# Attention and routed experts on one core: the last batch's attention interleaved with the first sort, and the order of writes and fillers changed

## The chip, the cores and the metric

One NeuronCore of a Trainium2 chip runs the whole kernel. The metric is the device time of one execution in microseconds; lower is better. The engines are TensorE (PE), VectorE (DVE), ScalarE (ACT), GpSimd (POOL) and SyncE (SP). DMA transfers are issued from the queues of SP, ACT and POOL, and each engine carries out its own instructions strictly in the order in which the program lists them.

## What is computed

The input is x (4 batches of 256 rows, 256 columns, float32), a context of 4 x 256 x 128 and two gates. Two residual steps follow each other:

```python
query = ctx @ Wq.T + bq;  key = ctx @ Wk.T + bk
attention = softmax(query @ key.T)
x = x + tanh(g_xattn) * (layernorm(x) @ attention.T)      # per batch

z = layernorm(x)
probs = softmax(gelu(z @ rw1) @ rw2)                      # 8 experts
wgt, idx = top_k(probs, 2)
for e in range(8):
    Ye = gelu(z @ w1[e] + b1[e]) @ w2[e] + b2[e]          # 256 -> 1024 -> 256
    Ce = gelu(b1[e]) @ w2[e] + b2[e]
    for k in range(2):
        mask = idx[..., k] == e
        out += any(mask) * wgt[..., k] * where(mask, Ye, Ce)
x = x + tanh(g_ffn) * out
```

Since a row that did not choose an expert still gets Ce, the kernel adds the same constant to every row (the sum of active * Ce, weighted by the row's two weights) and lets the experts' rows contribute Ye - Ce. The difference is made in the hidden layer: gelu(b1) is subtracted from gelu(z w1 + b1) before the second product.

## The kernel before

**First stage** (the text `order`, L433). Batches 0, 1 and 2 (1024 rows in all are 8 tiles of 128; these are tiles 0 to 5) go through attention, layer norm and router. Each word of `order` is a step from the table `steps` (L428), such as `qk:1` (the projections of batch 1) or `xf:2a` (normalize tile 4). The schedule is manual: the order of the words is the order on every engine. The steps that the change touches: `st` (L303, bn_stats for the first layer norm, VectorE), `pw`/`pf` (L306, L351, its power -0.5 on POOL), `xn` (L309, normalize), `tra`/`xnT` (transposes on TensorE, copy on ScalarE), `en`, `nmax`, `exp`, `norm`, `pt`, `attT` (energy, row maximum, exponential, division by the sum, transposes and their copy), `po` (product of attention and normalized rows), `add` (L342, residual, and the write of the rows to the output), `sf`/`xf` (second layer norm; `xf`, L354, also writes the normalized rows to the scratch `rows` in DRAM), `trf`, `xT`, `r`, `gel`, `lg` (router), `chosen` (which two experts a row takes). `w2:n` puts the next n loads of w2 (1 MB each) on SP's queue. Tanh, Exp and Gelu need different activation tables on ScalarE, and a table is loaded when a function needs it that the present one lacks.

**First sort.** The 1536 (row, expert) pairs of tiles 0 to 5 are sorted by expert into slots of 128 pairs of one expert each. NA = 5 full slots can be filled before batch 3 is known. `cnt`, `pc`, `scan`, `over`, `runs`, `lead`, `rank`, `pos`, `split`, `put` count and place the pairs with small VectorE instructions and TensorE products; `hqs_inv` (12 one-hot compares on VectorE, 24 small products on TensorE) turns the positions into the slots' lists; `lists` makes row numbers of them, `past` and `who` the expert of each slot, `sel` and `bias_` the slots' biases. `soft`, `wgt` and `piece` make the softmax weights. Batch 3's attention steps are placed between these (L910 to L920).

**Slots.** For each slot, POOL gathers 128 normalized rows from `rows` (L745), TensorE transposes them (`turn`, L753; the copy xs is on ScalarE for slots 0 to 4, on VectorE after), `first_layer` (L768, here F0, F1 ...; F1.3 is its fourth chunk of eight) multiplies by w1 of the slot's expert, which SP has loaded (`fill`, 1 MB, six buffers), ScalarE applies Gelu and VectorE subtracts gelu(b1). `second_layer` (L790, here S0, S1 ...) multiplies by w2, VectorE scales the result (ys) and POOL adds it to the output rows by an indirect DMA (L801). TensorE runs F0, turn 1, turn 2, F1, S0, turn 3, F2, S1, and so on. Tiles 6 and 7 are sorted with what the first sort left over (second sort, slots 5 on); this data uses 19 slots, of which 16 are in the fixed part and the rest under branches.

**Fillers.** After every chunk of F or S the function `between` (L957) is called with 0.45 of credit (less after the chunks that carry VectorE work). It takes the next items of two lists and puts their instructions at that place in every queue: `main` (L932: batch 3's router, second sort, biases, then the bias path: for each expert e a row b2 is loaded into one of two buffers by `b2_`, L811, and eight `bias_path` and two `both_` instructions on VectorE add up the constants; `sums1_`, L854, sums them over partitions with one TensorE product called cst; then `constant_row` for each tile and `add_constants`) and `second` (L954: the weights of the first sort's slots). A number in a list is a break of so many calls. Items with a cost wait until the credit is not negative.

A few lines carry the rest of the working:

```python
    def hidden(name, shape=(P, IC, P), dtype=F32):                                   # L461
        return slotp.tile(list(shape), dtype, tag="hT", bufs=6, name=name)
        go.hqs = hidden(f"hqs{i}", (P, go.ng, P), BF16)                              # L627
        if e < 2:                                                                    # L813
            nc.gpsimd.memset(b2_row[e], 0.0)
        nc.sync.dma_start(out=b2_row[e % 2][0:1, :], in_=b2[e : e + 1, :])
            if s > NA:                                                               # L978
                gather_to(s + AHEAD)
            if 0 < s < NA - 2:
                fill_to(s + 2)
```

`slotp` is opened after the pools of the first stage have been closed and lies in their memory.

Of the kernel before, what the change touches and what calls it, by code (L numbers as in the profile page):

```python
# [19 lines left out]
def gated_xattn_moe_kernel(  # L20
# [25 lines left out]
    P = 128  # L46
# [105 lines left out]
    nc.gpsimd.dma_start(out=g_sb, in_=gates[0].partition_broadcast(P))  # L152
# [105 lines left out]

    def norm(b):
        att, den = live["att", b], live["den", b]  # L260
        rden = small.tile([P, NN], F32, tag="rden", name=f"rden_{b}")
        nc.vector.reciprocal(rden, den)
        for m in range(NN):
            nc.vector.tensor_scalar(  # L264
                att[:, m, :], att[:, m, :], rden[:, m : m + 1], tg[:, 0:1], ALU.mult, ALU.mult
            )
# [26 lines left out]
    def normal(kind, key, tiles, dst):  # L293
        mv, rstd = live["ln", kind + key]
        for i, t in enumerate(tiles):
            nc.vector.tensor_scalar(
                dst[:, i, :], acc[:, t, :], mv[:, i, 0:1], rstd[:, i : i + 1], ALU.subtract, ALU.mult
            )
# [10 lines left out]
    def xn(b):  # L309
        normal("a", b, rows_of(b), made("xn", b, [P, LT, D]))  # L310
# [31 lines left out]
    def add(g):  # L342
# [3 lines left out]
        nc.sync.dma_start(out=in_rows(total, g), in_=xb)  # L346
# [61 lines left out]
    def tbl(_):  # L408

        nc.scalar.activation(warm, ones[:, 0:1], AF.Tanh)  # L410

# [12 lines left out]

    def w2_(n):
# [5 lines left out]
        chosen=chosen, tbl=tbl, ident=ident_, masks=masks, w2=w2_,  # L431
    )
    order = """  # L433
        w2:5 tbl ident qk:0 st:0 qk:1 tg q:0 k:0 pw:0 st:1 qk:2 k:1 q:1 xn:0 pw:1 st:2 en:0 k:2 q:2 tra:0 nmax:0 pw:2
        en:2 xnT:0 xn:1 exp:0 en:1 nmax:2 tra:1 xn:2 exp:2 norm:0 tra:2 xnT:1 norm:2 pt:0 xnT:2 masks nmax:1 pt:2
        attT:0 exp:1 po:0 attT:2 norm:1 po:2a add:0 pt:1 sf:0 po:2b attT:1 add:2a po:1 pf:0 add:2b sf:2a xf:0 w2:1
        pf:2a add:1 trf:0 sf:2b xT:0 sf:1 pf:2b r:0 gel:0 xf:2b w2:1 pf:1 xf:2a w2:1 trf:2b lg:0 xT:2b trf:2a xf:1
        r:2b xT:2a chosen:0 trf:1 gel:2b r:2a xT:1 lg:2b gel:2a chosen:2b r:1 lg:2a gel:1 chosen:2a lg:1 chosen:1
# [22 lines left out]
    def hidden(name, shape=(P, IC, P), dtype=F32):  # L461
        return slotp.tile(list(shape), dtype, tag="hT", bufs=6, name=name)
# [50 lines left out]
    nc.gpsimd.memset(runs2[:, 0:1], 0.0)  # L513

# [106 lines left out]
    def put_(i):  # L621
# [5 lines left out]
        go.hqs = hidden(f"hqs{i}", (P, go.ng, P), BF16)  # L627
# [43 lines left out]
    def soft_(i):  # L671
# [5 lines left out]
        nc.gpsimd.tensor_tensor(flat, euler.to_broadcast([P, n * E]), flat, ALU.pow)  # L677
# [90 lines left out]
    def first_layer(s, hT, between=nothing):  # L768
# [5 lines left out]
        for ch in range(IC):  # L774
# [13 lines left out]
            between(0.45 - (0.69 if ch % 4 == 3 else 0.0))  # L788

    def second_layer(s, hT, between=nothing):  # L790
# [4 lines left out]
        for i in range(IC):  # L795
            nc.tensor.matmul(ps[:, 0:D], lhsT=hT[:, i, :], rhs=w2_sb[:, i, :], start=(i == 0), stop=(i == IC - 1))  # L796
            between(0.45 - (0.9 if i == IC - 1 else 0.0))
# [111 lines left out]
    with tc.manual_schedule(engines=MANUAL):  # L909
        do("cnt:0 pc:0 scan qk:3 soft:0 over:0 runs:0 lead:0 q:3 k:3 rank:0 pos:0 split:0 en:3 put:0")  # L910
        hqs_inv(0)
        do("past:0 who:0 fill:0 lists:0 gather:0 nmax:3 exp:3 st:3 gather:1 pw:3 gb1 fill:1 sel:0")
        bias_(0, 0, 0, NA)
        do("norm:3 pt:3 xn:3 attT:3 tra:3 xnT:3 gather:2")
        bias_(0, 1, 0, NA)
        do("po:3 wgt:0 add:3")
        for v in range(3):
            piece_(0, v)
        turn(0, transposed_rows(0))
        do("sf:3 pf:3 gather:4 fill:2")  # L920
# [8 lines left out]
        def f(cost, fn, *a):  # L929
# [3 lines left out]
            w(.65, "xf:3"), 2, w(0, "trf:3"), w(0, "xT:3"), 2, w(0, "r:3"), w(0, "gel:3"), 2, w(0, "lg:3"), 1,  # L933
            w(1.6, "chosen:3"), w(.25, "cnt:1"), 2, w(0, "pc:1"), w(.42, "scan"), w(.5, "soft:1"), w(.9, "over:1"),
            w(.35, "runs:1"), w(.8, "lead:1"), w(.5, "rank:1"), w(1.25, "pos:1"), w(.9, "split:1"), w(.6, "put:1"),
        ]
        for g in range(0, G, 4):
# [4 lines left out]
            1, w(.6, "lists:1"), w(.45, "past:1"), w(.6, "who:1"), w(0, "gather:8 fill:7"), w(.25, "sel:1"),  # L942
        ]
        third = XS // 3
        main += [f(1.1, bias_, 1, i, 0, third) for i in range(2)] + [w(1.0, "wgt:1")]
# [121 lines left out]
```

## Time and profile before

| | |
|---|---|
| runs | 216.37, 215.63, 216.63, 213.5 us; median 216.0 |
| profiled execution | 214.05 us, of which the span is 212.3 |
| TensorE busy | 181.7 us (86%), mean granted clock 0.939 |
| VectorE busy | 143.1 us (67%) |
| ScalarE busy | 78.9 us (37%) |
| GpSimd busy | 80.3 us (38%) |
| first h of slot 0 | 53.82 us |
| last ys ends | 204.28 us |

The page divides the span into 40 slices of 5.3 us; a digit is the busy share of a slice in tenths, and the line PEclk is the clock granted to TensorE, 9 being full speed and 5 half. The chain that ended last gives start, length and the work or the wait in order of time. The timeline gives start, length, engine, line, operation and, in brackets, how long the engine had been idle before it and what ended that. SPq, ACTq and POOLq are DMA issues.

### The profile page before, as it was taken

How to read it: one execution, taken by the hardware profiler on the slowest of the kernel's cores; microseconds unless marked ns; L12 is line 12 of the kernel's file. 1: busy time of each engine (PE TensorE's matmuls, PEld its weight loads, DVE VectorE, ACT ScalarE, POOL GpSimd, SP SyncE). 2: the span in 40 equal slices, each digit the busy share in tenths (PEclk: the TensorE clock that was granted, in tenths of full speed). 3: DMA queues.
4: the chain of work that ended last, by engine and by line, in shares of the span. 5: the costliest groups of instructions: out<-in, count | busy, mean ns of one | idle time of the engine just before them, and what ended most of it. 6: DMA issues, size and time to landing. Idle time of an engine off the chain costs nothing.

```text
span 212.3 us, 3829 instructions
## 1 busy us (share of the span) xinstructions
PE 181.7 (86%) x1198; PEld 160.0 (75%) x1198; DVE 143.1 (67%) x419; ACT 78.9 (37%) x205; POOL 80.3 (38%) x89
## 2 busy tenths in 40 slices
PE   3699784728499999699999999999999999999930
PEld 2577472416389989589899999999989989999820
DVE  2777989593637778879858999999988742243200
ACT  2275441071265516135135324532532452354100
POOL 7210314971313507704061246423440430566230
PEclk9999995555999999999999999999999999999995
DMA  5999999157596014990647979759662249332221
GB/s 158 259 321 352 356 373 367 49 170 300 189 304 254 6 23 82 369 277 18 194 104 256 330 260 247 240 183 350 180 206 44 47 48 152 49 55 35 50 29 20
DMA packets 23576, 38.76 MB, mean 183 GB/s; under 512 B 2328, under 2 KB 17696, under 8 KB 23552
## 3 DMA queue, kind: packets, MB, share of 16 engines
q1 hardware_dynamic: 18208, 32.16, 43.8%
q0 software_dynamic: 4912, 6.17, 17.2%
q8 instruction: 13, 0.21, 0.4%
q10 hardware_dynamic: 432, 0.13, 0.3%
q14 instruction: 11, 0.09, 0.1%
HBM read 33.21 MB, written 5.64 MB: 183 GB/s over the span
## 4 chain that ended last, share of the span: by engine, by line
PE 59%; DMA 17%; DVE 11%; issue 6%; POOL 2%; ACT 1%; SPq 0%; POOLq 0%; DVEq 0%; ACTq 0%
PE h L777 25%; PE y L796 23%; DMA out<-ys,give 8%; DMA rows<-xf 4%; DMA xg<-rows,take 3%; DMA ctx_sb<-in_ctxT 3%; PE po L331 2%; PE qk L224 2%; PE xt L760 2%; POOL out L801 1%; DVE att L264 1%; DVE acc L345 1%; DVE nmax L247 1%; DVE st_f L284 1%; DVE hqs L632 1%
## 5 line engine op out<-in xcount | busy, mean ns | idle before, releaser
L781 ACT ACTIVATE hT<-h,bsel 128x128 f32<-128x128 f32 x152 | 55.9, 368 | 74.1 <-PE h L777 56.6
L777 PE MATMUL h<-xs,w 128*128 128x128 f32 x608 | 72.2, 276 | 0.5 <-ACT xs L762 0.5
L777 PEld LDWEIGHTS h<-xs,w 128*128 128x128 f32 x608 | 69.9, 192 | 1.3 <-ACT xs L762 0.7
L796 PE MATMUL y<-w_all,hT 128*128 x304 | 70.1, 381 | 0.6 <-issue 0.6
L796 PEld LDWEIGHTS y<-w_all,hT 128*128 128x128 f32 x304 | 56.0, 190 | 7.7 <-issue 0.9
L801 POOL DMA_INDIRECT out<-ys,give x14 | 22.8, 1630 | 52.5 <-DVE ys L799 29.9
L784 DVE TENSOR_TENSOR hT<-hT,gbsel 128x512 f32<-128x512 f32 x38 | 26.2, 689 | 20.7 <-ACT hT L781 18.8
L823 DVE SCALAR_TENSOR_TENSOR gsum<-w_all,gb,gsum 128x256 f32<-128x256 f32 x56 | 27.1, 484 | 1.6
L745 POOL DMA_INDIRECT xg<-rows,take x23 | 25.3, 1102 | 7.5 <-issue 3.4
L799 DVE TENSOR_SCALAR ys<-y,share 128x256 f32<-128x256 f32 x19 | 9.1, 481 | 14.7 <-PE y L796 11.6
L801 POOL DMA_INDIRECT out<-ys,take x5 | 8.8, 1753 | 22.5 <-DVE ys L799 14.3
L677 POOL TENSOR_TENSOR prob<-euler,prob 128x48 f32<-128x48 f32 (+1 forms) x2 | 10.9, 5468 | 14.6 <-DVE capped L569 7.4
L760 PE MATMUL xt<-ident,xg 128*128 128x128 f32 x40 | 7.8, 278 | 2.3 <-DMA xg<-rows,take 1.8
L291 POOL TENSOR_TENSOR rstd_f<-rstd_f,halves 128x2 f32<-128x2 f32 x3 | 2.1, 712 | 18.7 <-DVE rstd_f L286 18.7
L760 PEld LDWEIGHTS xt<-ident,xg 128*128 128x128 f32 x40 | 5.6, 145 | 4.8 <-issue 2.3
L331 PE MATMUL po<-attT,xnT 128*128 128x256 f32 x24 | 7.8, 478 | 0.7 <-ACT xnT L324 0.7
L224 PE MATMUL qk<-ctx_sb,wq_sb 128*128 128x256 f32 x6 | 3.5, 682 | 5.2 <-DMA ctx_sb<-in_ctxT 5.2
L762 DVE COPY xs<-xt 128x256 f32<-128x256 f32 x15 | 6.3, 418 | 1.6 <-PE xt L760 0.6
L331 PEld LDWEIGHTS po<-attT,xnT 128*128 128x128 f32 x24 | 5.4, 236 | 2.3 <-ACT xnT L324 1.1
L272 PE MATMUL pt<-ident,att 128*128 128x128 f32 x16 | 3.2, 327 | 4.3 <-DVE att L264 4.2
L762 ACT COPY xs<-xt 128x256 f32<-128x256 f32 x5 | 1.9, 371 | 12.5 <-PE xt L760 12.5
L632 DVE TENSOR_SCALAR hqs<-rowb,qf 128x128 bf16<-128x128 bf16 x28 | 4.8, 249 | 2.5 <-DMA rows<-xf 2.5
(200 smaller groups left out, 179.2 us busy)
## 6 DMA issues: line engine op xcount, KB each, us to landing
w<-in_w SPq DMA_DIRECT2D x18, 1024.0 KB, 7.7
w_all<-in_w SPq DMA_DIRECT2D x8, 1024.0 KB, 11.8
acc<-in_x SPq DMA_DIRECT2D x4, 256.0 KB, 5.7
w<-in_w SPq DMA_DIRECT2D x2, 512.0 KB
out<-acc POOLq DMA_DIRECT2D x1, 1024.0 KB
out<-acc SPq DMA_DIRECT2D x3, 256.0 KB, 7.3
rows<-xf SPq DMA_DIRECT2D x3, 256.0 KB
ctx_sb<-in_ctxT SPq DMA_DIRECT2D x3, 128.0 KB
```

The source lines that it names most:

```text
L331: nc.tensor.matmul(ps[:, ts(i, N)], lhsT=live["xnT", b][:, n, ts(t % LT, P)], rhs=live["attT", b][:, n, :], start=(n == 0), stop=(n == NN ...
L677: nc.gpsimd.tensor_tensor(flat, euler.to_broadcast([P, n * E]), flat, ALU.pow)
L745: nc.gpsimd.indirect_dma_start(out=xg, out_offset=None, in_=rows[0 : EARLY * P if s < NA else T, :], in_offset=bass.IndirectOffsetOnAxis(a ...
L760: nc.tensor.transpose(ps[:, ts(c, P)], xg[:, ts(c, P)], ident)
L762: copy(xs, ps[:, 0:D].rearrange("p (c l) -> p c l", c=DC))
L777: nc.tensor.matmul(ps[:, 0:P], lhsT=w1_sb[:, c, ts(ch, P)], rhs=xs[:, c, :], start=(c == 0), stop=(c == DC - 1),)
L781: nc.scalar.activation(hT[:, ch, :], ps[:, 0:P], AF.Gelu, bias=bias[:, ch : ch + 1])
L784: nc.vector.tensor_tensor(hT[:, part, :], hT[:, part, :], gbias[:, part].rearrange("p (i o) -> p i o", o=1).to_broadcast([P, 4, P]), ALU.s ...
L796: nc.tensor.matmul(ps[:, 0:D], lhsT=hT[:, i, :], rhs=w2_sb[:, i, :], start=(i == 0), stop=(i == IC - 1))
L799: nc.vector.tensor_scalar(ys, ps[:, 0:D], go.share[:, j : j + 1], None, ALU.mult)
L801: nc.gpsimd.indirect_dma_start(out=total[0:last_row, :], out_offset=bass.IndirectOffsetOnAxis(ap=go.give[:, j : j + 1], axis=0), in_=ys, i ...
L823: nc.vector.scalar_tensor_tensor(gsums[e], w2_all[:, e, c, :], gb1[:, e, c : c + 1], b2_row[e % 2] if c == 0 else gsums[e], ALU.mult, ALU.add)
```

## The change

1. The gates' load leaves POOL's queue for ScalarE's; the tanh of the gates (`tg`) moves from ahead of `q:0` to behind `q:2`. `tbl` becomes `table:NAME`, which can load any table: Tanh at the start, Exp at the end of the first stage, Gelu ahead of the slots.
2. `add` no longer writes the output rows. A new step `ow` does, and stands at the end of the first stage (for batch 3: behind `add:3`). The last three w2 loads move behind `xf:1`'s write of the normalized rows.
3. Batch 3: `st:3 pw:3 xn:3` move into the first stage (with `xn:3` on POOL), `qk:3`, `q:3`, `k:3` and gelu(b1) to its end, and transposes, energy, maximum, exponential, division and the transposes of the attention between the first sort's steps. Its division is made on ScalarE, by reciprocals that VectorE has multiplied by the gate (`rden`).
4. hqs0 gets memory of its own (`hqs1` in pool `last`); hT has five buffers instead of six.
5. The first sort's exponential is on ScalarE; `soft:0` moves behind the lists.
6. Ahead of slot 0 only slot 0's biases are made; those of slots 1 to 4 go into `second`. `fill:2` is no longer issued ahead of slot 0, and gathers 2 to 4 stand behind `pf:3`.
7. Fillers: other costs, longer breaks in batch 3's router, `past:1 who:1` ahead of the second sort's places, smaller deductions of credit, items of `main` released down to a credit of -1, and marks by which an item must have been put in place.

The diff, cut to its core:

```diff
-    nc.gpsimd.dma_start(out=g_sb, in_=gates[0].partition_broadcast(P))
...
+    def rden(b):
+        live["rden", b] = rden_ = small.tile([P, NN], F32, tag="rden", name=f"rden_{b}")
+        nc.vector.reciprocal(rden_, live["den", b])
+        if b == "3":
+            nc.vector.tensor_scalar(rden_, rden_, tg[:, 0:1], None, ALU.mult)
+
     def norm(b):
+        att = live["att", b]
+        if b == "3":
+            for m in range(NN):
+                nc.scalar.activation(att[:, m, :], att[:, m, :], AF.Copy, scale=live["rden", b][:, m : m + 1])
+            return
+        rden(b)
...
     def xn(b):
-        normal("a", b, rows_of(b), made("xn", b, [P, LT, D]))
+        normal("a", b, rows_of(b), made("xn", b, [P, LT, D]), nc.gpsimd if b == "3" else nc.vector)
...
-        nc.sync.dma_start(out=in_rows(total, g), in_=xb)
+
+    def ow(g):
+        nc.sync.dma_start(out=in_rows(total, g), in_=acc[:, spread(g), :])
...
     order = """
-        w2:5 tbl ident qk:0 st:0 qk:1 tg q:0 k:0 pw:0 st:1 qk:2 k:1 q:1 xn:0 pw:1 st:2 en:0 k:2 q:2 tra:0 nmax:0 pw:2
+        w2:5 table:Tanh g ident qk:0 st:0 qk:1 q:0 k:0 pw:0 st:1 qk:2 k:1 q:1 xn:0 pw:1 st:2 en:0 k:2 q:2 tg tra:0 nmax:0 pw:2
         en:2 xnT:0 xn:1 exp:0 en:1 nmax:2 tra:1 xn:2 exp:2 norm:0 tra:2 xnT:1 norm:2 pt:0 xnT:2 masks nmax:1 pt:2
-        attT:0 exp:1 po:0 attT:2 norm:1 po:2a add:0 pt:1 sf:0 po:2b attT:1 add:2a po:1 pf:0 add:2b sf:2a xf:0 w2:1
-        pf:2a add:1 trf:0 sf:2b xT:0 sf:1 pf:2b r:0 gel:0 xf:2b w2:1 pf:1 xf:2a w2:1 trf:2b lg:0 xT:2b trf:2a xf:1
-        r:2b xT:2a chosen:0 trf:1 gel:2b r:2a xT:1 lg:2b gel:2a chosen:2b r:1 lg:2a gel:1 chosen:2a lg:1 chosen:1
+        attT:0 st:3 pw:3 xn:3 exp:1 po:0 attT:2 norm:1 po:2a add:0 pt:1 sf:0 po:2b attT:1 add:2a po:1 pf:0 add:2b sf:2a xf:0
+        pf:2a add:1 trf:0 sf:2b xT:0 sf:1 pf:2b r:0 gel:0 xf:2b pf:1 xf:2a trf:2b lg:0 xT:2b trf:2a xf:1 w2:3
+        r:2b xT:2a chosen:0 trf:1 gel:2b r:2a xT:1 lg:2b gel:2a chosen:2b r:1 lg:2a qk:3 gel:1 gb1 table:Exp q:3 k:3
+        chosen:2a lg:1 chosen:1 ow:0 ow:2a ow:2b ow:1
     """
...
-        return slotp.tile(list(shape), dtype, tag="hT", bufs=6, name=name)
+        return slotp.tile(list(shape), dtype, tag="hT", bufs=5, name=name)
...
+    hqs1 = last.tile([P, GA, P], BF16, name="hqs1")
...
-        go.hqs = hidden(f"hqs{i}", (P, go.ng, P), BF16)
+        go.hqs = hqs1 if i == 0 else hidden(f"hqs{i}", (P, go.ng, P), BF16)
...
-        nc.gpsimd.tensor_tensor(flat, euler.to_broadcast([P, n * E]), flat, ALU.pow)
+        if i == 0:
+            nc.scalar.activation(flat, flat, AF.Exp)
+        else:
+            nc.gpsimd.tensor_tensor(flat, euler.to_broadcast([P, n * E]), flat, ALU.pow)
...
-            between(0.45 - (0.69 if ch % 4 == 3 else 0.0))
+            between(0.45 - (0.6 if ch % 4 == 3 else 0.0))
...
-            between(0.45 - (0.9 if i == IC - 1 else 0.0))
+            between(0.45 - ((0.4 if s < NA else 0.8) if i == IC - 1 else 0.0))
...
-        do("cnt:0 pc:0 scan qk:3 soft:0 over:0 runs:0 lead:0 q:3 k:3 rank:0 pos:0 split:0 en:3 put:0")
+        do("cnt:0 tra:3 pc:0 scan en:3 xnT:3 over:0 runs:0 nmax:3 lead:0 exp:3 rank:0 pos:0 split:0 rden:3 put:0 norm:3 pt:3 attT:3")
         hqs_inv(0)
-        do("past:0 who:0 fill:0 lists:0 gather:0 nmax:3 exp:3 st:3 gather:1 pw:3 gb1 fill:1 sel:0")
-        bias_(0, 0, 0, NA)
-        do("norm:3 pt:3 xn:3 attT:3 tra:3 xnT:3 gather:2")
-        bias_(0, 1, 0, NA)
-        do("po:3 wgt:0 add:3")
+        do("past:0 who:0 fill:0 lists:0 gather:0 sel:0 soft:0 po:3 gather:1 fill:1")
+        for i in range(2):
+            bias_(0, i, 0, 1)
+        do("wgt:0 add:3 table:Gelu ow:3")
+        turn(0, transposed_rows(0))
+        do("sf:3 pf:3 gather:4")
         for v in range(3):
             piece_(0, v)
-        turn(0, transposed_rows(0))
-        do("sf:3 pf:3 gather:4 fill:2")
...
-            w(.65, "xf:3"), 2, w(0, "trf:3"), w(0, "xT:3"), 2, w(0, "r:3"), w(0, "gel:3"), 2, w(0, "lg:3"), 1,
-            w(1.6, "chosen:3"), w(.25, "cnt:1"), 2, w(0, "pc:1"), w(.42, "scan"), w(.5, "soft:1"), w(.9, "over:1"),
-            w(.35, "runs:1"), w(.8, "lead:1"), w(.5, "rank:1"), w(1.25, "pos:1"), w(.9, "split:1"), w(.6, "put:1"),
+            3, w(.65, "xf:3"), 3, w(0, "trf:3"), 1, w(0, "xT:3"), 3, w(0, "r:3"), w(0, "gel:3"), 3, w(0, "lg:3"), 1,
+            w(1.4, "chosen:3"), w(.2, "cnt:1"), 4, w(0, "pc:1"), w(.35, "scan"), w(.3, "soft:1"), w(.7, "over:1"),
+            w(.3, "runs:1"), w(.5, "past:1"), w(.5, "who:1"), w(.45, "lead:1"), w(.4, "rank:1"), w(1.3, "pos:1"),
+            w(.75, "split:1"), w(.6, "put:1"),
...
-        second = [2] + [f(0, inw_, 0, g) for g in range(GA)] + [1, w(.25, "share:0")]
+        second = [f(.6, bias_, 0, i, 1, 2) for i in range(2)] + ["biases 1"]
+        second += [f(1.2, bias_, 0, i, 2, NA) for i in range(2)] + ["biases 2"]
+        second = [5] + [f(0, inw_, 0, g) for g in range(GA)] + [2, w(.25, "share:0"), "shares 0"] + second
...
+                    if isinstance(queue[0], tuple) and queue[0][0] > 0 and credit < (-1.0 if name == "main" else 0.0):
                         break
```

## The prediction

> **What bounds the kernel now.** I read the page, then the chain that ended last, then the timeline of 20–110 us and of the stretch where the constants are summed, then busy time by windows of 1 us.
>
> From the page:
> ```profile
> span 212.3 us, 3829 instructions
> PE   3699784728499999699999999999999999999930
> PEclk9999995555999999999999999999999999999995
> ```
> From 53 us on TensorE is full but for one notch; before that it has a hole (slices 6 to 11) in which its clock is half. By the windows the clock falls at 32.6 us and is back at 53.1. The chain in order of time shows what fills the hole:
> ```profile
> 30.48 9.21 DMA rows<-xf
> ...
> 39.98 2.04 DVE hqs L632 x12
> ...
> 49.30 3.79 PE po L331 x8
> ...
> 81.91 6.17 DMA xg<-rows,take
> ```
> The first is a false dependency: hqs0 is carved from memory that xf held, so VectorE waits until the last rows have been written (2.51 us idle before 39.98), behind 8 MB of w2 and the output rows on SP's queue. Then batch 3's attention runs alone until slot 0 starts at 53.82. The fourth line is the notch: TensorE waits 1.76 us for the gather of slot 5. From slot 4 on every slot takes 7.25 us of TensorE (118.69, 125.94, 133.18 in the timeline).
>
> A third place matters, the bias path's constants, in the timeline:
> ```profile
> 105.14 0.48 DVE L799 TENSOR_SCALAR ys<-y,share 128x256 f32<-128x256 f32 x1
> 105.90 1.56 POOL L801 DMA_INDIRECT out<-ys,take  x1 [4.96 <-DVE ys L799]
> 107.77 1.01 POOL L745 DMA_INDIRECT xg<-rows,take  x1 [0.30 <-PE h L777]
> 109.08 1.05 POOL L745 DMA_INDIRECT xg<-rows,take  x1 [0.30 <-issue]
> 110.14 0.33 POOL L814 MEMSET b_row<- 128x256 f32 x1
> 110.49 0.29 SPq L815 DMA_DIRECT2D b_row<-in_b  x1
> 111.97 0.49 DVE L823 SCALAR_TENSOR_TENSOR gsum<-w_all,gb,b_row 128x256 f32<-128x256 f32 x1 [2.43 <-issue]
> ...
> 157.51 1.10 PE L856 MATMUL cst<-both,ones 128*128 128x512 f32 x2
> ```
> The second b2 row is cleared on POOL behind a scatter and two gathers, so VectorE stands for 2.43 us. Afterwards it runs late: ys at 121.63 belongs to a product that ended at 118.85 (2.8 us late), ys at 155.76 to one that ended at 155.09 (0.7 late). It has just caught up when cst needs it. No slack is left there.
>
> **Part by part: up to slot 0.** All times are estimates, worked out from rows of before.
>
> st:3 enters VectorE's first stage: 1.33 us (43.24 to 44.57) into a wait of 1.09 (17.72 to 18.80), so +0.25. pw:3 (0.72) and xn:3 go to POOL ahead of pf:0, which starts at 21.83: POOL is free from about 20.0, and pf:0 may start at 22.7 before xf:0 is late, so xn:3 has 2.7 us. POOL runs no such operation before. Bounds: two clears of 128x256 at 0.33 give 0.7 us; two at the rate of the power in L677 (8.01 us for 48 columns) give 85. I take 1.5, nearer the clear, since subtract and multiply are no power; hidden. GPSIMD Engine Reference, section Engine selection, calls POOL the wrong engine here, about twice VectorE's time; twice the 0.41 of a VectorE row would be 1.6 for both, an estimate that fits the hole too.
>
> The gates' load leaves POOL's queue (0.77) for ACT's (0.45), and tg moves from 6.81 to after q:2; ACT idles there and norm:0 needs tg only at 15.26: nothing.
>
> qk:3 goes in front of lg:1 on TensorE. lg:2a ends at 31.1, qk:3 takes 1.8 (9.07 to 10.78), lg:1 0.5: chosen:1 starts at 33.5 instead of 32.04. With the 0.25, +1.45: cnt:0 at 35.0 instead of 33.50. gb1, the Exp table (1.28 + 0.2), q:3 and k:3 on ACT end at 34.0, before en:3.
>
> Then VectorE: scan, over, runs to 36.1 (0.36 less, soft:0 is gone from here); en:3 on TensorE 35.45 to 37.2 (1.70 at full clock, 2.07 at half); nmax to 37.9; lead to split 2.19; rden 0.35; put 0.37: 40.8. The wait for the rows is gone, hqs starts at once: 42.8; past and who: 43.4 (now 42.57). So the sorting does not get shorter: what the wait gave up, qk:3, en:3 and nmax take. norm:3 on ACT and pt:3 end at 42.0, the 24 inv at most 0.085 each later: the list stands at 43.5 to 44.1 (now 42.6). soft:0's power (8.01 on POOL) becomes an ACT exp under 0.5; POOL was idle anyway: nothing.
>
> What follows is shorter. Rows go ahead of w2:3 and the outputs, whose 4.2 MB from 28.3 on at 0.365 MB/us end near 40, before the gather; the four ow issues (0.4 each on SP) end by 33, before fill:0. Gather 0 starts 0.9 after the list (as now, 43.50): 44.6. Now its bytes pass between 47 and 48, 4.7 us after the start, beside the fills: 49.3. Turn and copy 0.95 (52.87 to 53.82): **slot 0 at 50.2, 3.6 earlier.** po:3 (44.0 to 47.8 at half clock), add:3 (0.69), sf:3 (1.27), pf:3 (0.97) lie beside that and end at 50.8; gather 2, now behind pf:3 on POOL (51.0, landing by 54.2), is just in time for turn 2 at 55. ow:3 and the later fill 2 are hidden: fill 2 is due at slot 2.
>
> Clock: now it rises at 53.1, after 3.8 us of po:3. If po:3 does not lift it, F0 runs at half speed for up to 3 us, +1.5 (nothing if it does). I take nothing and keep 1.5 for the range. TensorE: Matmul & The Clock Gate, Part 1, gives a free-running window of 3.4 us, so its phase may differ by run; by that rule about half the runs would pay.
>
> **Slots 0 to 5.** Now slot 1 starts at 63.49 and slot 2 at 71.0, because xf:3 waits for pf:3 (56.42) and PE stops for trf, r, lg in turn. With pf:3 done early and pauses of 3, F0 costs 3.57 + 0.7 (trf, inw); then turn 1, turn 2, and 1.1 for ACT's xT:3 and xs copies: F1 at 56.35. F1 with r and lg 4.85, S0 with pc 3.55, turn 0.2: slot 2 at 65.0 (6.0 earlier). VectorE gets the bias of slots 1 to 4 (2.55 us) here. Its list from add:3 to lists:1 sums to 20.1 us in some 23 of TensorE, so it is nearly the bound: 0.85 is lost before the first inv. Slot 3 at 73.3, the list at 77.0. Gather 5 starts at 77.3; who:1 now stands before the sort's end, so SP issues fills 5 to 7 near 66 and their 3 MB are through by 76 (1 MB in 2.9 us at 0.36 MB/us, the rate of 20 to 30 us); it lands at 80, before turn 5 at 81.0: **the notch of 1.76 is gone**, slot 4 at 81.25 (now 88.62). But piece 2 ends at 85.0 and inw comes at F4.4 (83.5): 1.45 back, what is late next. Slot 5 at 90.6 (96.98), slot 6's turn at 98.0, ys of slot 4 ends at 99.2 (105.62): **6.4 gained there.** One buffer less in hT costs nothing: hqs0 no longer takes one and hT_s is reused five allocations later, when slot s is long over.
>
> **What is given back.** The row's chain after that ys is unchanged: 0.28 + 1.56 + 0.30 + 1.01 + 0.30 + 1.05 + 0.04 + 0.33 + 1.5 = 6.4: b2's row lands at 105.55. From there 70 items at 0.467 (10 more slots' items: a slot of 6.63 has 10, one of 7.03 has 11) and 12.2 of ys, xs and hT: 45 to 45.4 (now 111.97 to 157.36). both is ready at 150.9, 6.4 earlier. But the filler now releases faster: credit per slot is 7.2 - 1.2 - 0.8 = 5.2 instead of 7.2 - 1.38 - 0.9 = 4.92, and main may go to -1, so cst is queued on TensorE after product S11.3 instead of F13.4. TensorE is there at 147.0 (slot 6 at 98.0 + 6 x 7.25, + 5.5) and waits 3.9 us. Behind cst it has 4.2 us more work than now (S11.4 to 7, a turn, F13.0 to 4). Net 6.4 - 4.1 = 2.3 to 2.4. The constant rows and their write then come earlier, and the last scatter's chain (205.14 to 205.88) is the same.
>
> Sum: span 212.3 - 2.4 = 209.9. The profiled execution took 214.05, 1.95 less than the median of the runs, 216.0; the middle of these five executions is 215.6. I set the sum against that: 215.6 - 2.4 = **213.2 us**.
>
> **Rivals.**
> - The early start stays whole: VectorE is not late at cst, since the b2 row lands sooner or the items run faster. For: from 120 to 140 us VectorE is busy 19.36 of 20 us and holds nobody up; against: the row's chain above. 215.6 - 6.4 = 209.2.
> - Nothing to measure: half clock in F0 (1.5) and a gather that lands a microsecond later leave 4 at slot 6, all given back at cst: 215.6. For: from 46 to 50 us TensorE was busy 2.85 of 4 us and the clock stayed at half; against: po:3 follows inv without a gap.
> - Slower: xn:3 on POOL holds up pf:0. It decides from 2.7 us for the pair; each microsecond beyond goes into the VectorE chain, and from 5.1 on the 2.4 are gone. At 4 us each: 8 - 2.7 = 5.3 against 2.4, so 215.6 + 2.9 = 218.5. For: POOL's arithmetic rows are slow (0.72 us for two columns); against: the clears.
>
> **How the numbers follow.** Chances: forecast 0.47, whole gain 0.25, nothing 0.18, slower 0.10. The forecast's own range is 211.5 to 215 (1.5 for the clock, 1.5 to 2 for the waits estimated in slots 1 to 4). For eight in ten I go from 208.3 (the whole gain and 0.9) to 217.5, leaving out the worse half of the slow case and the very best. About 1% (2.2 us) is what a measurement here can tell from no change. Faster by more needs under 213.8: some 0.6 of the forecast's 0.47 (0.28), nearly all of the second (0.24), a little of the third (0.05): 0.57. Slower by more, over 218.2: most of the last and a trace of the third: 0.11. The same: 0.32.
>
> **What would show it.** Right: no wait before hqs; cnt:0 near 35, slot 0's first h near 50, slot 2 near 65; no wait of xt for slot 5; VectorE idle some 4 us before the second b2 row, and TensorE standing 3 to 4 us before cst. Wrong: cst without a wait (then near 209), a first h after 52, or xn:3 beyond 1.3 us each with pf:0 late behind it.

## The result, and the profile after

| | before | after |
|---|---|---|
| median of the runs | 214.17 us (212.5 to 217.57, 70 runs) | 213.53 us (212.05 to 214.34, 44 runs) |
| profiled execution | 214.05 us, span 212.3 | 214.36 us, span 212.5 |
| TensorE busy, mean clock | 181.7 us, 0.939 | 182.1 us, 0.941 |
| GpSimd busy | 80.3 us | 72.6 us |
| first h of slot 0 | 53.82 us | 47.46 us |
| constants' product (cst) | 157.51 us, no wait | 150.71 us, after a wait of 4.66 |

The ratio of the runs is 0.9981, 95% interval 0.9966 to 0.9995: some 0.4 us less, within the 1% that the prediction counts as no change. 213.2 us was predicted; that is near 213.53, but only because the sum was set against 215.6 and the runs of before have their middle at 214.17. The predicted difference, -2.4 us, was several times the measured one, and the predicted span, 209.9, was 2.6 us too short. Some executions of any of these kernels are longer by some per cent; the ratios leave out those more than 1.5% above the fastest of their kernel, the medians do not. The profiled execution of after, 214.36 us, is longer than any of its 44 runs, so the spans and waits read below are those of a long one.

The page of the kernel after, the lines that answer to those shown of before:

```profile
span 212.5 us, 3835 instructions
PE   3999763929899997999999999994699999999940
PEclk9999999557999999999999999999679999999995
```

Counted from 1, the early hole is shorter (slices 6 to 9), the notch of slice 17 is gone, and slices 28 and 29 have a new hole, with a new loss of clock in 29 and 30. That hole holds most of the answer. The timeline of after (start, length, engine, line, operation; in brackets the idle time before it and what ended it), the early stage and the place of the hole:

```profile
18.06 2.45 POOL L304 TENSOR_SCALAR xn<-acc,mv_a,rstd_a 128x256 f32<-128x256 f32 x2
28.90 0.68 PE L223 MATMUL qk<-ctx,wq_sb 128*128 128x256 f32 x2
36.86 2.04 DVE L648 TENSOR_SCALAR hqs<-rowb,qf 128x128 bf16<-128x128 bf16 x12
39.12 3.78 PE L339 MATMUL po<-attT,xnT 128*128 128x256 f32 x8
40.42 1.22 POOL L764 DMA_INDIRECT xg<-rows,take  x1 [14.96 <-DMA out<-acc]
46.34 0.66 PE L779 MATMUL xt<-ident,xg 128*128 128x128 f32 x2 [3.43 <-issue]
47.46 4.59 PE L796 MATMUL h<-xs,w 128*128 128x128 f32 x24 [0.46 <-ACT xs L781]
...
80.30 0.38 PE L779 MATMUL xt<-ident,xg 128*128 128x128 f32 x2
84.08 0.59 PE L727 MATMUL inw<-putw,hqs 128*128 128x54 bf16 x16 [1.17 <-DVE putw L719]
...
105.58 0.48 DVE L842 SCALAR_TENSOR_TENSOR gsum<-w_all,gb,b_row 128x256 f32<-128x256 f32 x1 [4.07 <-DMA b_row<-in_b]
...
144.16 1.89 PE L815 MATMUL y<-w_all,hT 128*128 x8
150.71 2.05 PE L875 MATMUL cst<-both,ones 128*128 128x512 f32 x2 [4.66 <-DVE both L851]
152.55 3.62 PE L815 MATMUL y<-w_all,hT 128*128 x8
```

Read the last three rows first. TensorE stands 4.66 us for VectorE's constants, and then the same eight records of y that took 1.89 us before the wait take 3.62 behind it; cst takes 2.05 (1.10 in the kernel before). The windows of one microsecond say why (the figure before the last two is the granted clock):

```profile
149.00:150.00 1.00, 0.00 (x0) 0.00 (x0) 0.96 (x3) 0.00 (x0) 0.69 (x2) 0.96 0.80 328
150.00:151.00 1.00, 0.29 (x1) 0.32 (x2) 0.56 (x2) 0.00 (x0) 1.00 (x1) 0.50 0.78 136
156.00:157.00 1.00, 1.00 (x7) 1.00 (x6) 0.79 (x3) 0.00 (x0) 0.03 (x1) 0.62 0.00 0
```

The clock falls to half at 149.9, 3.9 us after TensorE's last work, and is back at 156.8. So in these two rows behind the wait 0.95 + 1.73 = 2.7 us are lost to half clock, and in the turn and the first products behind them, up to 156.8, another 0.3: from cst to the start of the next second layer it takes 9.43 us here (150.71 to 160.14), and 6.48 at full clock in experiment 3 (151.09 to 157.57).

**Where the time went, by the starts of the slots' turns on TensorE.** Slot 2 is 6.2 us earlier than before (64.42 against 70.61), slot 5 is 7.9 (80.30 against 88.21), slot 7 is 7.4 (96.78 against 104.19). At cst 4.66 go to the wait and 2.95 to the half clock, and at 175.49 the y waits 0.69 where it waited 0.35: 7.41 - 4.66 - 2.95 - 0.34 = -0.54. The last scatter starts 0.44 later than before (206.32 against 205.88). Of the 7.4 some 1.2 is no work of the change: the second projection started at 7.21 in the profiled execution of before and at 5.67 in that of after, and in a profiled execution of nearly the kernel before (with one clear moved, below) it started at 5.95 and slot 7 at 102.95. Against that one the lead is 6.2. Counted from the second projection, the profiled execution of after is even the longer one by 1.7 us (212.5 - 5.67 against 212.3 - 7.21), while the runs differ by 0.4 the other way: single executions do not settle the last microsecond or two.

### The profile page after: what moved, and what is told of

Its sections match the earlier page's. It is cut to its first block, busy times and chain, and to the rows that moved or that the text cites. A ratio compares the mean times of both kernels' runs of the same rounds, so it can differ in the third digit from the quotient of the medians.

```text
span 212.5 us, 3835 instructions
## 1 busy us (share of the span) xinstructions
PE 182.1 (86%) x1198; PEld 161.5 (76%) x1198; DVE 142.6 (67%) x424; ACT 80.0 (38%) x210; POOL 72.6 (34%) x89
## 4 chain that ended last, share of the span: by engine, by line
DVE 20%; PE 18%; issue 13%; DMA 5%; POOL 2%; SPq 1%; POOLq 0%; DVEq 0%
DVE gsum L842 11%; PE h L796 8%; PE y L815 8%; DVE hT L803 4%; DMA out<-ys,give 4%; DVE both L851 2%; POOL out L820 2%; DVE ys L818 1%; PE cst L875 1%; DVE xs L781 1%; DMA out<-ys,take 1%; DMA b_row<-in_b 1%; PE xt L779 1%; POOL xg L764 0%; SPq L893 0%
## 5 line engine op out<-in xcount | busy, mean ns | idle before, releaser
L796 PE MATMUL h<-xs,w 128*128 128x128 f32 x608 | 74.9, 280 | 0.6 <-ACT xs L781 0.5
L796 PEld LDWEIGHTS h<-xs,w 128*128 128x128 f32 x608 | 72.0, 196 | 1.4 <-ACT xs L781 1.2
L815 PE MATMUL y<-w_all,hT 128*128 x304 | 71.2, 387 | 0.7 <-issue 0.7
L815 PEld LDWEIGHTS y<-w_all,hT 128*128 128x128 f32 x304 | 57.3, 194 | 9.0 <-issue 1.9
L764 POOL DMA_INDIRECT xg<-rows,take x23 | 24.1, 1048 | 22.8 <-DMA out<-acc 15.0
L696 POOL TENSOR_TENSOR prob<-euler,prob 128x16 f32<-128x16 f32 x1 | 2.9, 2934 | 13.6 <-DVE capped L585 13.6
L842 DVE SCALAR_TENSOR_TENSOR gsum<-w_all,gb,b_row 128x256 f32<-128x256 f32 x8 | 3.9, 481 | 4.7 <-DMA b_row<-in_b 4.7
L299 POOL TENSOR_TENSOR rstd_a<-rstd_a,halves 128x2 f32<-128x2 f32 x4 | 3.0, 752 | 11.3 <-DVE rden L260 6.6
L781 ACT COPY xs<-xt 128x256 f32<-128x256 f32 x5 | 1.8, 372 | 13.2 <-PE xt L779 13.2
L851 DVE SCALAR_TENSOR_TENSOR both<-gsum,act,both 128x256 f32<-128x256 f32 x14 | 6.3, 482 | 0.2
```

Of the source, the lines that this page charges most:

```text
L764: nc.gpsimd.indirect_dma_start(out=xg, out_offset=None, in_=rows[0 : EARLY * P if s < NA else T, :], in_offset=bass.IndirectOffsetOnAxis(a ...
L781: copy(xs, ps[:, 0:D].rearrange("p (c l) -> p c l", c=DC))
L796: nc.tensor.matmul(ps[:, 0:P], lhsT=w1_sb[:, c, ts(ch, P)], rhs=xs[:, c, :], start=(c == 0), stop=(c == DC - 1),)
L842: nc.vector.scalar_tensor_tensor(gsums[e], w2_all[:, e, c, :], gb1[:, e, c : c + 1], b2_row[e % 2] if c == 0 else gsums[e], ALU.mult, ALU.add)
L851: nc.vector.scalar_tensor_tensor(both[:, k, :], gsums[e], a, both[:, k, :], ALU.mult, ALU.add)
```

## The experiments

Times are medians of the runs; "ratio" is to the kernel before, run beside it on the same chip (before: 215.04, 214.48 and 214.75 us on three chips). One execution of 374.9 us of the first kernel of the table and one of 471.05 us of the kernel before are left out of these medians. Spans are those of the one profiled execution of each kernel.

| kernel | time | ratio, 95% interval | span |
|---|---|---|---|
| after, both b2 rows cleared early | 206.98 | 0.9597 (0.9483 to 0.9712) | 206.0 |
| after, longer break ahead of cst | 206.56 | 0.9586 (0.9474 to 0.9698) | 205.5 |
| after, TensorE kept busy through the wait | 211.49 | 0.9825 (0.9732 to 0.9918) | 209.8 |
| after, TensorE kept busy ahead of slot 0 | 211.89 | 0.9857 (0.9798 to 0.9916) | 210.8 |
| after, early clear and busy ahead of slot 0 | 204.96 | 0.9548 (0.9506 to 0.9590) | 203.2 |
| the last, and a break of 6 ahead of cst | 205.22 | 0.9578 (0.9530 to 0.9627) | 203.2 |
| after, xn:3 on VectorE | 214.65 | 1.0006 (0.9964 to 1.0048) | 213.1 |
| after, old allowances of the fillers | 218.66 | none (215.06 to 219.67) | 217.8 |
| before, both b2 rows cleared early | 214.38 | 0.9996 (0.9955 to 1.0038) | 211.0 |
| before, gates' load on ScalarE's queue | 214.53 | 1.0015 (0.9967 to 1.0064) | 211.8 |
| before, early rows and own hqs0 | 213.05 | 0.9938 (0.9901 to 0.9974) | 211.8 |
| the last, and soft:0 on ScalarE | 212.12 | 0.9897 (0.9834 to 0.9961) | 210.6 |

**1. The second b2 row.** The theory was that its late load makes the wait at cst.

```diff
-        if e < 2:
-            nc.gpsimd.memset(b2_row[e], 0.0)
+        if e == 0:
+            nc.gpsimd.memset(b2_row[0], 0.0)
+            nc.gpsimd.memset(b2_row[1], 0.0)
```

> The changed kernel, with both b2 buffers cleared on POOL at the first expert, so that the second row's load no longer stands behind a scatter and two gathers. Theory 1 (the start's gain is given back at cst, because VectorE stood 4.07 us for that row): VectorE goes on at 101.4 instead of 105.6, both is ready near 146.4, TensorE waits under 0.7 us ahead of cst, its clock stays up, and the wait of 4.66 and the 2.7 us at half clock behind it are gone: 7 us less than the changed kernel, about 206.5. Rival (VectorE is the bound through the whole bias path, the row's wait only shows it): cst still waits 3 us or more and the time falls by under 2 us.

The timeline of that kernel:

```profile
102.41 0.47 DVE L843 SCALAR_TENSOR_TENSOR gsum<-w_all,gb,b_row 128x256 f32<-128x256 f32 x1
147.55 1.10 PE L876 MATMUL cst<-both,ones 128*128 128x512 f32 x2 [0.53 <-DVE both L852]
```

The row is there without a wait, cst waits 0.53 us and runs at full clock. The span, 206.0, is what the prediction's first rival gives (212.3 - 6.4 = 205.9): with this wait away the early gain stays whole. The rival, VectorE as the bound through the whole bias path, falls.

**2. The place of cst.** The row stays late; TensorE is given other work in front of cst.

```diff
-        main += [2, f(0, sums1_, 0), 2, f(.8, sums2_, 0)]
+        main += [14, f(0, sums1_, 0), 2, f(.8, sums2_, 0)]
```

> The changed kernel with a break of 14 instead of 2 calls ahead of cst, nothing else: the row's wait on VectorE stays, but cst is queued on TensorE some 5.4 us of work later. Theory 1: TensorE does its products meanwhile and does not wait; 7 us less than the changed kernel, about 206.5, the same as with the early clear. Rival (VectorE's backlog is what ends last, wherever cst stands): no change beyond 1 us, since the constant rows come later by as much.

VectorE still stands 4.08 us for the second row, at 105.12, but the timeline has no wait at cst:

```profile
150.96 1.02 PE L875 MATMUL cst<-both,ones 128*128 128x512 f32 x2
```

The clock is 1.00 through the place. So the late row costs nothing by itself; it costs where a product that needs its sum stands too early in TensorE's order.

**3. The wait without the half clock.** Twenty 128x128 products that nothing uses stand on TensorE ahead of cst (here, and where such products come again below, they are work that the reference does not have).

```diff
+        for _ in range(20):
+            nc.tensor.matmul(live["cst", 0][:, 0:P], lhsT=ident, rhs=ones, start=True, stop=True)
```

> The changed kernel with 20 products of 128x128 float32 (some 4.4 us at full clock, their results overwritten) put on TensorE directly ahead of cst. They add work and compute nothing. Theory 1a (the half clock after the wait is caused by the wait, and costs 2.7 us): cst and the four products behind it run at full clock, the time falls by 2 to 3 us, to about 211. Rival 1b (the clock falls for another reason, or its cost is hidden): no gain, or a loss of up to 1 us.

The timeline:

```profile
146.37 4.63 PE L876 MATMUL cst<-ones,ident 128*128 128x128 f32 x40
151.09 1.12 PE L877 MATMUL cst<-both,ones 128*128 128x512 f32 x2
152.05 1.89 PE L815 MATMUL y<-w_all,hT 128*128 x8
```

cst starts no earlier than in the kernel after, but it takes 1.12 us and the eight y take 1.89, at a clock of 1.00. The span is 209.8, 2.7 less. The forecast span was 209.9: this is the kernel that the prediction's sum described, the wait without its aftermath.

**4. Is the row worth anything in the kernel before?** The diff of 1, made to the kernel before.

> The kernel before with both b2 rows cleared at the start of the bias path, so that VectorE no longer stands 2.43 us for the second one. Theory (before, the constants' product stands on TensorE where VectorE has just been in time; the b2 row alone is worth nothing there): 0 to 0.5 us less than before, ratio 0.997 to 1.001, the wait at the second b2 row gone, the constants' product still near 157. Rival (the b2 row's chain is on the path of the kernel before too, so that clearing it early is a gain of its own): 2 to 2.4 us less, ratio 0.989.

Ratio 0.9996. There cst stands behind F13.4 and comes at 156.2 with no wait, so clearing early gains nothing:

```profile
156.19 1.10 PE L857 MATMUL cst<-both,ones 128*128 128x512 f32 x2
```

The span, 1.3 us shorter than that of the kernel before, is the earlier start of this execution (second projection at 5.95 against 7.21). The wait at cst is the change's own.

**5. The old allowances of the fillers,** the prediction's reason for cst having moved forward.

```diff
-            between(0.45 - (0.6 if ch % 4 == 3 else 0.0))
+            between(0.45 - (0.69 if ch % 4 == 3 else 0.0))
-            between(0.45 - ((0.4 if s < NA else 0.8) if i == IC - 1 else 0.0))
+            between(0.45 - (0.9 if i == IC - 1 else 0.0))
-... credit < (-1.0 if name == "main" else 0.0):
+... credit < 0.0:
```

> The changed kernel with one part undone: the filler's old allowances per slot (0.69 and 0.9 held back, and the main list may not go below zero). It puts the constants' product on TensorE some 8.6 us of TensorE's own work later (behind the seventh product of slot 12's second layer, not the fourth of slot 11's). Theory (the wait before that product, and the half clock after it, is what takes the early gain back; it comes from the order of the work, not from the b2 row being late as such): no wait before the constants' product, clock 1.00 from 140 to 160 us, the second b2 row's wait still about 4 us, and 205.5 to 207.5 us. Rival (the wait moves to the next product that needs VectorE or to the tail): 210 us or more. Rival (the early slots lose by slower fillers, so that the notch before slot 5 is back): the wait is gone but slot 6 starts 1 to 2 us later, 207.5 to 209.

This expectation failed. The four runs lie between 215.06 and 219.67 us and the profiled one is the longest, so only what the order of the work forces is read. From its timeline:

```profile
81.68 1.13 POOL L764 DMA_INDIRECT xg<-rows,take  x1 [4.84 <-DVE pad L664]
86.46 0.41 PE L779 MATMUL xt<-ident,xg 128*128 128x128 f32 x2 [3.44 <-DMA xg<-rows,take]
121.08 0.48 DVE L842 SCALAR_TENSOR_TENSOR gsum<-w_all,gb,b_row 128x256 f32<-128x256 f32 x1 [3.97 <-DMA b_row<-in_b]
166.36 2.04 PE L875 MATMUL cst<-both,ones 128*128 128x512 f32 x2 [3.51 <-DVE both L851]
```

The second list is 5.2 us later (its gather at 81.68, 76.43 in the kernel after), so the notch before slot 5 is back at 3.44 us (1.9 of the 5.2 are already there at slot 0's turn, 48.28 against 46.34, ahead of every filler); the first b2 row waits 4.04 us as well as the second 3.97; and VectorE's sums come so much later that cst waits 3.51 us at its later place too. So undoing the allowances does not by itself take the wait away: cst comes later, and VectorE's sums come later too. That the new allowances carry the second sort in time is read from this one long execution, and what they are worth in the others is not shown. The second rival (the notch is back) had that direction, but I had priced it at 1 to 2 us and without a wait at cst.

**6. The half clock in slot 0.** Eight unused products between po:3 and slot 0's turn, alone and with the diff of 1.

```diff
+        held = bank_x("held")
+        for _ in range(8):
+            nc.tensor.matmul(held[:, 0:P], lhsT=ident, rhs=ones, start=True, stop=True)
         turn(0, transposed_rows(0))
```

> The changed kernel with both b2 rows cleared at the start of the bias path (as in the run with the early clear) and eight 128x128 products that nothing uses on TensorE between the last batch's output projection and the turn of slot 0, in its idle time of some 3 us. Theory (slot 0's first layer runs at half clock because TensorE stood idle before it; that costs 1.6 to 2 us, which move everything behind it): slot 0's first layer at 0.22 us or less per product pair row of the timeline, first h at the same time as without, slot 1 1.5 to 2 us earlier, span 204 to 204.6 against 206.0 with the early clear alone. Rival (the extra products are too short to lift the clock, or slot 1 waits for its rows): slot 1 less than 0.5 us earlier, span 205.5 to 206.

> The changed kernel with the eight unused 128x128 products in TensorE's idle time ahead of slot 0's turn, and nothing else; the second b2 row is late as in the changed kernel. Theory (VectorE's chain through the b2 row starts from slot 4's scaled product, so what is won before slot 4 moves the constants' product and TensorE's arrival at it alike, and the wait there stays 4.6 us long and is followed by half clock again): slot 1's layers 2.4 to 3 us earlier, the wait before the constants' product 4 to 5.3 us, span 209.5 to 210.3 against 212.5, and about 2.4 us less in the runs than the changed kernel's 213.5. Rival (the wait at the constants' product takes whatever is won before it): the wait grows to 7 us or more, span 212 to 212.5.

The timeline with these products alone:

```profile
42.94 3.05 PE L934 MATMUL held<-ones,ident 128*128 128x128 f32 x16
47.59 2.94 PE L796 MATMUL h<-xs,w 128*128 128x128 f32 x24 [0.46 <-ACT xs L781]
149.20 2.04 PE L875 MATMUL cst<-both,ones 128*128 128x512 f32 x2 [4.65 <-DVE both L851]
```

Slot 0's 24 records take 2.94 us instead of 4.59 (5.33 in the kernel of 1). With the early clear the span falls by 2.8, from 206.0 to 203.2 (204.0 or more was expected), 2.4 of it by this clock. Alone, they make slot 1's turn 1.5 us earlier (53.30 against 54.81; 2.4 to 3 was expected), and the wait at cst stays 4.65 us long. The span is 1.7 shorter, 0.5 less than expected; the runs' ratio against that of the kernel after (0.9857 to 0.9981) gives 1.2%, 2.7 us, with 1.4 to 3.9 inside the interval. What is won before slot 4 moves VectorE's chain and TensorE alike, and passes through the wait. The rival, that the wait takes it, falls.

**7. A longer break on top of both** (6 in place of 2 ahead of cst).

> The changed kernel with three additions: both b2 rows cleared at the start of the bias path, a pause of 6 filler steps (not 2) ahead of the constants' product, and the eight unused products ahead of slot 0's turn. Theory (the three waits are separate, the first two act on the same place): as with the early clear and the unused products (span 203.2) less the last wait of 0.7 us before the constants' product: span 202.3 to 203, runs 204 to 205, ratio 0.950 to 0.957. Rival (the later product delays the constant rows and their write, which then end last): span 203.5 or more.

cst comes without a wait, and the last scatter starts 1.0 us earlier (195.77 against 196.79), but the span is the same 203.2, between the theory's range and the rival's, and so are the runs within their intervals. Behind that last scatter no engine has any more work recorded; why the end comes 7.4 us after its start, and 6.4 without the longer break, stays open. Both versions are the fastest of the study, some 8 to 9 us below the kernel after.

**8. xn:3 back on VectorE.**

```diff
-        ..., nc.gpsimd if b == "3" else nc.vector)
+        ..., nc.vector)
```

> The changed kernel with the last batch's first normalization back on VectorE (two operations of some 0.4 us there in place of two of 1.2 us on GpSimd). Theory (on GpSimd it lies beside other work; on VectorE it stands in the stage's longest chain): first count of the sort 0.4 to 0.8 us later against its start, 0 to +0.8 us in all, 213.5 to 214.4. Rival (GpSimd was the wrong engine for it, about twice VectorE's time, and its queue held up the normalizations' powers): pf:0 0.5 us earlier and the sort's first count 0.4 us or more earlier, 212.5 to 213.2.

VectorE waits 0.81 us for the powers and then takes 0.74 for the pair; xf:0 starts at 22.71 instead of 21.24, the sort's first count comes 1.5 us later (33.34 against 31.86; 0.4 to 0.8 was expected), and cst 2.3 later than in the kernel after. The last scatter is only 0.5 later, since here the half clock behind cst costs 1.7 us, not 3.0, and the 0.69 at 175.49 is gone. The rival falls: pf:0 comes 1.1 us later, not earlier. In the runs the two can't be told apart. GpSimd was the right place for the stage, and worth little at the end.

**9. What opened the early stage.** The gates' load alone, made to the kernel before (it goes onto ScalarE's queue, tg behind q:2):

> The kernel before with the first part of the change alone: the gates' load on ACT's queue instead of POOL's, and the tanh of the gates behind q:2. Theory 2 (the 1.8 us by which the changed kernel's first stage is ahead, from the second projection at 5.67 against 7.21 on, come from this load): the second projection starts below 6 us and the time falls by about 1.5 us, to 212.6. Rival (the landing of the first loads varies from run to run): the second projection still starts near 7 us in some executions, and the median stays.

The second projection starts at 5.59 us (7.21), but in three other executions that keep the load on GpSimd's queue it starts at 5.80, 5.95 and 6.49: the early start does not need this edit, and the runs don't move (1.0015). Then the rows' write ahead of outputs and late w2, with hqs0 in memory of its own:

> The kernel before with two small parts of the change alone: the normalized rows' write ahead of the output rows and the late second-layer weights on SyncE's queue, and the first list's one-hot products in memory of their own. The last batch's attention stays where it was. Theory (before, the wait of 2.51 us for the rows delays VectorE's list and the attention behind it by as much; the attention's output projection, not the gather, then releases slot 0): hqs without wait, first h at 51 to 51.8 (before 53.8), 2 to 2.5 us less at slot 6, and at the end 1.5 to 2.5 us less, since the constants' product stands late in the order: ratio 0.988 to 0.993. Rival (the rows' wait was hidden behind the gather or the attention): first h after 53, ratio 0.997 to 1.001.

hqs runs without a wait, first h is at 50.48. Of these 3.3 us against the kernel before some 1.4 are the start of the execution (second projection at 5.80 against 7.21); the kernel of experiment 4, which started at 5.95, has its first h at 52.29. The timeline shows two covers that the prediction had not seen:

```profile
32.09 8.01 POOL L681 TENSOR_TENSOR prob<-euler,prob 128x48 f32<-128x48 f32 x1 [7.21 <-DVE prob L679]
40.30 1.20 POOL L749 DMA_INDIRECT xg<-rows,take  x1 [0.19 <-DMA out<-acc]
86.23 0.41 PE L764 MATMUL xt<-ident,xg 128*128 128x128 f32 x2 [3.19 <-DMA xg<-rows,take]
86.47 5.36 PE L781 MATMUL h<-xs,w 128*128 128x128 f32 x32
```

The list is ready at 37.5, but GpSimd is in the power of soft:0 until 40.1; and what is won ahead of slot 0 turns into a longer notch before slot 5 (3.19 us, 1.76 before). Behind it the 32 records of h take 5.36 us, 3.74 in the kernel before: the clock was half from 87.38 to 90.79. In the runs 1.3 us are left (0.9938; 0.988 to 0.993 was expected). With soft:0 as an exponential on ScalarE:

```diff
+        if i == 0:
+            nc.scalar.activation(flat, flat, AF.Exp)
+        else:
             nc.gpsimd.tensor_tensor(flat, euler.to_broadcast([P, n * E]), flat, ALU.pow)
```

> The kernel before with the rows' early write, the first list's one-hot products in memory of their own, and the first softmax's exponential on ScalarE in place of the power on GpSimd (8.01 us). The prediction put that move at nothing, as GpSimd was idle. Theory (it is the next cover: without it the first gather starts at 40.3 though its list is ready at 37.5, and the last batch's power and normalization stand behind the gathers): first gather 0.3 to 0.9 us after its list, output projection of the last batch 1 to 2 us earlier and first h at 48.5 to 49.5 (50.48 without the move), slot 5's gather still late, so at the end no more than 1 us less: ratio 0.989 to 0.995. Rival (GpSimd's power hides behind the attention as it did before): first h at 50 to 50.8.

This execution started late (the sort's first count at 32.48, 31.09 without the move), so times are taken from that count: the gather 7.35 us behind it instead of 9.21, po:3 13.2 instead of 14.8, first h 17.8 instead of 19.4. The gather came 1.0 after its list; 0.9 was the most expected, and first h, at 50.32, is by its time from the span's start in the rival's range. The notch before slot 5, here 2.08 us, is again followed by half clock (h takes 5.36 us). The steps between agree with the theory, and the ratio 0.9897 with its range. How much of the lead of 6.2 us the moved attention of batch 3 brings by itself was not run alone.

## Why the prediction was right or wrong

**The step that failed is "What is given back": TensorE "is there at 147.0 ... and waits 3.9 us", then "net 6.4 - 4.1 = 2.3 to 2.4".** The mechanism was right nearly to the tenth: b2's row lands at 105.58 (predicted 105.55), VectorE stands 4.07 ("some 4"), cst starts at 150.71 (150.9), after a wait of 4.66 us, since TensorE was there at 146.05. The term was mis-sized: the wait was priced alone, and the half clock behind it was put at nothing. It is worth 2.7 us of span by experiment 3, and 209.9 + 2.7 = 212.6 against 212.5 measured. I had asked about the clock in F0 only. That the sum closes to a tenth is luck in part: the measured span is that of a long execution, and 1.2 us of its lead are its early start.

The Trainium skill, TensorE: Matmul & The Clock Gate, section Why this matters for your kernels, advises against idle gaps of TensorE beyond some 3 us. The wait I predicted, 3.9 us, was already longer. The traces agree for the wait at cst (in three kernels the clock fell 3.9, 3.1 and 4.9 us after TensorE's last work); but in the last kernel of experiment 9 half clock followed a wait of 2.08 us, so here shorter gaps cost too.

**Also wrong, in both directions:**
- "cnt:0 at 35.0". It came at 31.86. qk:3 took 0.95 us of TensorE's time, not 1.8: I priced it by rows of the first ten microseconds, where each of its two pairs of records takes 1.06 to 1.22 us. The start of the execution gave another 1.5. Of the remaining 0.7, 0.35 may be the idle time of TensorE ahead of lg:1 in the kernel before, which qk:3 fills; the rest stays open.
- The clock in F0, "I take nothing and keep 1.5". F0 ran at half clock in all six profiled executions with the changed order and no added products there, where the prediction gave about half of them, and that costs 1.6 to 2.4 us (4.55 to 5.37 for the 24 records, 2.94 with the added products). po:3 did not stand close ahead of turn 0, as I had it: it ended at 42.9, and TensorE then idled 3.43 us.
- First h at 50.2: 47.46. These errors cancel: 6.4 us early at ys of slot 4 was predicted, and ys ended at 99.2 as predicted. That is luck, since the start of the execution is among them.
- "soft:0 ... POOL was idle anyway: nothing". It was idle only as long as the rows were late; with the rows early the power holds up the first gather by some 2 us (experiment 9).

**Right:** no wait before hqs. xn:3 is hidden, though 1.2 us each instead of 0.75; the third rival, decided at 2.7 for the pair, was at 2.45, and pf:0 waited without making xf:0 late. The notch of 1.76 is gone, and the wait for putw before inw takes its place (1.45 predicted, 1.17 measured). One hT buffer fewer cost nothing that shows.

On the page of the Trainium skill that spoke against xn:3 on GpSimd (GPSIMD Engine Reference, section Engine selection): that section gives its factor of about two for operations with two inputs and calls one input roughly line-rate. This operation has a single input tensor, so the prediction misapplied the factor; the rows give three times VectorE's 0.41, and the measurement decides. Still, in experiment 8, the stage is 1.5 us shorter with it there, since the choice was between a busy and an idle engine.

**The rivals:** the whole gain kept (209.2) did not happen, but is what one moved clear makes of it. "Nothing to measure" is nearest to the result, by another road: its causes were the half clock of F0 and a late gather, and it was the half clock behind cst.

## What to carry to other kernels

A predicted wait of TensorE of some 2 us or more is to be priced with its aftermath: here 4.7 us of waiting cost 1.7 to 3.0 more at half clock, and 2.08 us of waiting cost 1.6. When one part of a schedule moves forward, follow the slowest chain of the other engines to the next product that needs it, and give that product's place in TensorE's order the same attention; one constant or one clear was worth 6 to 7 us here. And an edit costed at nothing "because the engine is idle" must be looked at again in the schedule after the change, where the work that hid it may be gone.

## What the runs showed of the hardware

- The projections of the first ten microseconds take 1.06 to 1.22 us for two records although the windows print a clock of 1.00 there; the first record of the clock in these traces comes only at 7.5 to 12.4 us (before 12.12, after 9.98). The same pairs take 0.68 and 0.59 at 28.90 in the kernel after, and 1.20 and 1.06 at 33.86 in the kernel before, at a printed 0.50. So here a row from the start of the program is a price at half clock.
- The clock changed in steps of 3.41 us: in all fourteen traces the time between two changes is a whole multiple of it. In the kernel after it is half from 37.29, full from 50.94, half from 149.93 and full from 156.75; 13.65, 98.99 and 6.82 us are 4, 29 and 2 times 3.413.
- What a wait costs goes with how it lies against these steps. Behind the same wait of 4.65 us the clock fell 3.9, 3.1 and 4.9 us after TensorE's last work and came back 6.0, 5.3 and 3.7 us after its next (the kernels after, with products ahead of slot 0, and with xn:3 on VectorE); the losses were 3.0, 2.6 and 1.7 us. At slot 5, waits of 2.08 and 3.19 us were followed by one step at half clock, waits of 1.76 and 2.01 by none.
- In the kernels of experiments 1 and 8, where a whole step lay within po:3, the clock came back at its end, at 42.70 and 44.04, and was lost again at 46.12 and 47.45 in TensorE's idle time ahead of slot 0. With the eight unused products there (1.95 to 3.05 us) it came back at 42.2 to 45.2 and stayed, in three executions.
- GpSimd takes 1.2 us for a subtract-and-multiply of 128x256 with two scalars per partition; VectorE takes 0.41.
- What spread the runs of the kernel before over 5 us, and those of after over 2.3, was not tried.
